# A graph-network layer: messages split around the factors, transfers asked for earlier, the last gate split by tokens

## Chip, cores, metric

One core of a Trainium2 chip runs the whole program, in one launch. The metric is the device time of that program in microseconds (us), median of several executions; lower is better.

## What is computed

The input is x, 32 batches of 512 tokens (nodes) with 256 features, and adj, a 512 by 512 adjacency of zeros and ones for each batch. All is float32. Cut to what matters:

```python
h = relu(layernorm(x))                                # per token
c = relu(bn1(conv1d(h^T, conv1_w)))                   # kernel width 1
c = bn2(conv1d(c, conv2_w, pad=8))                    # kernel width 17, along the tokens
x_conv = relu(c + h^T)^T
s = h @ w_se.T + b_se                                 # 3 features per token
A = exp(-|s_n - s_m|^2) * adj
msg = relu(h @ w_msg.T + b_msg)
x_nmp = A @ msg
gi = concat(x_conv, x_nmp) @ w_ih.T + b_ih            # 512 -> 3*256
gh = h @ w_hh.T + b_hh                                # 256 -> 3*256
r, z = sigmoid(gi_r + gh_r), sigmoid(gi_z + gh_z)
n = tanh(gi_n + r * gh_n)
out = x + (1 - z) * n + z * h
```

## The kernel before, in words

Tokens or features lie on the 128 partitions; 256 features are two chunks (DC = 2), 512 tokens four (NC = 4). The batches form two groups of 16 (GB = 16, NG = 2). For each group the kernel runs a first part and then the nodes; when both groups are done, the late part runs over 16 pairs of batches.

**First part** (`first_part`, manual order). For each batch: load x (`load_x`, most from POOL's queue), layer-norm statistics on VectorE (DVE) with a power on GpSimd (POOL) for rstd, normalise to `xn`, transpose on TensorE to `phT`, relu into `hT`, store `hT` to device memory as `hd` (SP's queue), conv1 as products `pc` into `h1`, and a transform of token windows to frequencies (`px`, copied to `xf`). In group 0 the steps between carry the conv2 weights to frequencies (`pw`, `wst`, `wd`) and load small weights. In group 1 they carry `combine_weights`: the three gate weight matrices are loaded in turn into one buffer `w` (bufs=1), combined on POOL (sums, L886 in the profile) and ScalarE (ACT, copies) into seven matrices each, and stored as `ws`. One step of that list runs per batch, from the second batch on: before the change a list of 13 steps, in which the load of the second and third matrix is the last entry of the step that ends the matrix before.

At the very start the queues are filled in this order: ACT asks for `vec` (vectors), `fwd` (forward transform), `taps`, and four pieces of w1 (`w_in`); SP asks for batch 0 (512 KB, one transfer), batch 1, and the first conv2 weights (`w2p`). TensorE meanwhile runs six products that nobody reads, into `row`. The batch-norm scale of conv1 is turned into rows (`bn1_row`: ACT copies, PE products) and multiplied into w1 by `scale_w1` on DVE.

**Nodes** (`nodes`). The order of the batches is `todo`: the last batch of the group first. `load_h` fetches h again, `by_chunks` copies it into another order (`hq`, ACT), `message` makes `msg` and the three s-features (products `pm`; DVE empties the banks, ACT applies the relu), `features` writes s and its squares into the shared tiles `fl` and `fr` (DVE), `factors` transposes them (`psl`, `psr`) and ACT copies them to `sl` and `sr`, `affinity` multiplies these (`pd`), takes exp on ACT into `e` and multiplies by the transposed adjacency on DVE into A, and `aggregate` makes `pn` from `msg` and A. In between, `product` does the frequency units of conv2 (`py` from weights `wt`, whose sum `wsum` and factor sums `both` POOL makes) and stores `yd`. Before the loop two batches are prepared under a manual order; inside the loop the framework's scheduler sets each engine's order from the program's order. All engines work their own queue strictly in order. `hT` has two slots, `adj` two, `hq` two, `wt` three.

**Late part** (manual order). For each pair of batches the conv2 result comes back from frequencies (`inverse`, `cp`), and the gates are made with a seven-product scheme (Q1 to Q7) in place of eight; `sums` on POOL builds the operands. For the last pair `last_z` runs after `gate_n`: seven products `pz` for z, then for each quarter (output half i, batch j of the pair) `gated` (add on DVE, sigmoid on ACT), `turned` (multiply and transpose on DVE) and `added` (add onto x on DVE), then `store`.

The hardware DMAs of SP and ACT share a set of completion counters, eight in turn, whatever queue they are issued from.

Of the kernel before, what the change touches and what calls it, by code (L numbers as in the profile page):

```python
# [11 lines left out]
FP = mybir.dt.float32  # L12
# [3 lines left out]
P = 128  # L16
# [49 lines left out]
def gnn_layer(  # L66
# [15 lines left out]
    nc = tc.nc  # L82
    B, N, D = x.shape
# [3 lines left out]
    DC = D // P  # L87
# [17 lines left out]
    def bank(name):  # L105
        return psum.tile([P, N], FP, tag="bank", name=name)
# [22 lines left out]
    nc.scalar.dma_start(vec, vecs)  # L129
    w1 = early.tile([P, DC, D], FP, name="w1")  # L130
    fwd = early.tile([P, 2 * L], FP, name="fwd")
    nc.scalar.dma_start(fwd, nc.inline_tensor(fwd_np, name="dft_fwd").ap())
    taps = early.tile([P, ROWS], FP, name="taps")
    nc.scalar.dma_start(taps, nc.inline_tensor(taps_np, name="dft_taps").ap())
    back = consts.tile([P, back_np.shape[1]], FP, name="back")
# [53 lines left out]
    def load_w1():  # L189

        t = W2P["w1"] = pools["gen"].tile([P, PI, D], FP, tag="w2p", name="w1_in", bufs=2)
        load_rows(t[:, :DC], w1T, nc.scalar)

    def scale_w1():
        t = W2P.pop("w1")
# [229 lines left out]
            nc.scalar.copy(chunks(HQ[b][:, ic, :]), by_chunk(HT[b][:, ic, :]))  # L425
        del HT[b]

    def message(b):
        MSG[b] = pools["nodes"].tile([P, NC, D], FP, tag="msg", name=f"msg_{b}", bufs=3)
        ST[b] = pools["nodes"].tile([P, 2, NC, NS], FP, tag="st", name=f"st_{b}", bufs=2)  # L430
        hq = HQ.pop(b)
        h = N // D
        for c0 in range(0, NC, h):
            m = MSG[b][:, c0 : c0 + h, :]
            for j in range(h):
                c = c0 + j
                p = bank(f"pm_{b}_{c}")
                for ic in range(DC):
                    nc.tensor.matmul(p[:, : D + NS], hq[:, ic, c * P : (c + 1) * P], wmsg[:, ic, :],  # L439
                                     start=(ic == 0), stop=(ic == DC - 1))  # L440
                nc.vector.tensor_add(ST[b][:, 0, c, :], p[:, D : D + NS], bmsg[:, D:])
                nc.vector.tensor_add(m[:, j, :], p[:, :D], bmsg[:, :D])
            nc.scalar.activation(m, m, AF.Relu)

    def features(b):

# [62 lines left out]
    def combine_weights():  # L509

        steps = []
        for k, src in enumerate((w_hhT, w_ihT[D:], w_ihT[:D])):
            w, t = (pools["sums"].tile([P, n, 3 * P], FP, tag=f"w{n}", name=f"w{n}_{k}", bufs=m) for n, m in ((4, 1), (7, 2)))
            rows = w.rearrange("p (c h) m -> p c (h m)", c=DC)
            load = (partial(nc.sync.dma_start, rows, src.rearrange("(c p) m -> p c m", p=P)) if k == 1 else
                    partial(load_rows, rows, src, nc.sync))
            if k == 0:
                steps.append([])
            steps[-1].append(load)

            a11, a21, a12, a22 = (
                w[:, 2 * c : 2 * c + 2].rearrange("p h m -> p (h m)").rearrange("p (g i o) -> p g i o", i=2, o=32)[:, :, i]
                for c in range(DC) for i in range(2)
            )
            q = [t[:, n].rearrange("p (g o) -> p g o", o=32) for n in range(7)]
            for (dst, x1, x2, op), kept in zip(
                ((Q5, a21, a22, ALU.add), (Q6, q[Q5], a11, ALU.subtract),
                 (Q7, a11, a21, ALU.subtract), (Q3, a12, q[Q6], ALU.subtract)),
                ((Q1, a11), (Q2, a12), (Q4, a22), None),
            ):  # L530
                steps.append([partial(nc.gpsimd.tensor_tensor, q[dst], x1, x2, op=op)])
                if kept:
                    steps[-1].append(partial(nc.scalar.copy, q[kept[0]], kept[1]))
            steps[-1].append(partial(nc.sync.dma_start, WS[k], t.rearrange("p q (g o) -> p q g o", o=P)))
        return steps
# [113 lines left out]
    def last_z(p, terms):  # L649

        d, o, ks = RZ[p], 1, range(K3)

        def gated(src, other, i, j, t=slice(0, N)):
            z, g = d[:, DC + i, j, t], DC + i
            if other is not None:
                nc.vector.tensor_add(z, other[:, t], src[:, t])
                src = z
            nc.scalar.activation(z, src, AF.Sigmoid, bias=brz[:, g : g + 1], scale=1.0)

        def places(i, t):  # L660
            return slice(t.start // 32, t.stop // 32), slice(32 * i, 32 * (i + 1))

        def turned(i, j, t=slice(0, N)):
            dst, (js, half) = d[:, i, j, t], places(i, t)
            nc.vector.tensor_mul(dst, dst, d[:, DC + i, j, t])
            if (p, j) not in OUT:
                OUT[p, j] = pools["late"].tile([P, N // 32, D // 4], FP, tag="o", name=f"o_{p}_{j}", bufs=2)
            nc.vector.transpose(OUT[p, j][:, js, half], dst.rearrange("p (j k) -> p j k", k=32))

        def added(i, j, t=slice(0, N)):  # L670
            js, half = places(i, t)
            x = XP[p][j][:, js, half]
            nc.vector.tensor_add(x, x, OUT[p, j][:, js, half])

        b1, b2, b3, b4, *b5 = (bank(f"pz{k}_{p}") for k in range(1, 7))
        into(b1, Q1, o, ks, terms, True)
        p1 = temp("p1", f"z{p}")
        nc.scalar.copy(p1, b1)
        into(b2, Q6, o, ks, terms, True)
        u2 = temp("u2", f"z{p}")  # L680
        nc.vector.tensor_add(u2, p1, b2)
        into(b1, Q2, o, ks, terms, False)
        gated(b1, None, 0, 0)
        early_out(p, 1, 1)
        turned(0, 0)
        into(b2, Q7, o, ks, terms, False)
        u3 = temp("u3", f"z{p}")
        nc.vector.tensor_add(u3, p1, b2)
        early_out(p, 0, 1)
        added(0, 0)  # L690
        into(b4, Q4, o, ks, terms, True)
        gated(b4, u3, 1, 0)
        into(b3, Q5, o, ks, terms, True)
        turned(1, 0)
        gated(b3, u3, 1, 1)
        nc.vector.tensor_add(u2, u2, b3)
        added(1, 0)
        store(p, 0, [nc.sync, nc.scalar])

        ts = [slice(h * N // 2, (h + 1) * N // 2) for h in range(2)]  # L700
        into(b5[0], Q3, o, ks, terms, True, ts[0])
        gated(b5[0], u2, 0, 1, ts[0])
        turned(1, 1)
        into(b5[1], Q3, o, ks, terms, True, ts[1])
        gated(b5[1], u2, 0, 1, ts[1])
        added(1, 1)
        for t in ts:
            turned(0, 1, t)
            added(0, 1, t)
            store(p, 1, [nc.sync, nc.scalar], t)  # L710
# [100 lines left out]
    def first_part(g, freq, between, left=()):  # L811
# [6 lines left out]
        if g == 0:  # L818
            t = XN[b0] = pools["first"].tile([P, NC, D], FP, tag="xn", name="rows", bufs=2)
            ones, diags = t[:, 0, :P], t[:, 1:3, :].rearrange("p i (c m) -> p i c m", m=P)  # L820
            nc.vector.memset(ones, 1.0)

            for _ in range(6):
                nc.tensor.matmul(row1[1][:, : 2 * P], ident, fr.rearrange("p c g k -> p (c g k)")[:, : 2 * P], start=True, stop=True)
            batch_norm("bn1", scale1, shift1, nc.gpsimd)
            bn1_row(0, scale1, ones, diags)
            bn1_row(1, shift1, ones, diags)
# [75 lines left out]
    with tc.tile_pool(name="freq", bufs=1) as fpool:  # L903
# [3 lines left out]
        with phase("first", "gen"):  # L907
            gen = pools["gen"]
            per = N // D
            steps = [partial(weights_to_freq, gen, pc, i) for pc in range(QI // PI) for i in range(0, PI, per)]  # L910
            load_w1()
            load_x(0)
            load_x(1)
            load_taps(gen, 0, nc.sync)

            def between(b):
                if b % 2 == 0 and b // 2 + 1 < QI // PI:
                    load_taps(gen, b // 2 + 1)
                if 1 <= b <= len(load_weights):
                    load_weights[b - 1]()  # L920
                mine = spread(steps, b, GB - 1) if b < GB - 1 else []
                return mine[:1], mine[1:]

            with tc.manual_schedule():
                xf = first_part(0, freq_tile, between)

                for u in range(3):
                    load_unit(0, u)
# [4 lines left out]
        def nodes(g, xf, units, last):  # L933
# [11 lines left out]
            load_adj(todo[0])  # L945
            with tc.manual_schedule():
                begin(0)
                message(todo[1])
                factors(todo[0])
                features(todo[1])  # L950
            affinity(todo[0])
            for i, b in enumerate(todo):
# [4 lines left out]
                    load_x(b1)  # L957
                if g + 1 < NG and i == 3 * GB // 4:
                    statistics(b1)
                if i + 2 < GB and todo[i + 2] not in HT:  # L960
                    load_h(todo[i + 2])
                if more:
                    load_adj(todo[i + 1])
                    factors(todo[i + 1])
# [4 lines left out]
                for u in mine[:1]:  # L969
                    product(pools["pw"], g, u, xf)  # L970
                begin(i + 2)
                if more:
                    affinity(todo[i + 1])
                for u in mine[1:2]:
# [109 lines left out]
```

## Time and profile before

| what | value |
|---|---|
| time, median of 7 runs (lowest, highest) | 1847.26 us (1844.19 to 1848.78) |
| profiled execution: time, span | 1848.72 us, 1846.9 us |
| mean granted TensorE clock | 0.995 |
| PE busy, instructions | 1825.8 us (99%), 6610 |
| DVE, ACT, POOL busy | 1110.3 (60%), 582.4 (32%), 588.2 us (32%) |
| group 0: first part, nodes | to about 165 us, to about 460 us |
| group 1: first part, nodes | to about 579 us, to about 880 us |
| late part | from about 880 us to the end |
| last PE product ends, last DVE instruction ends | 1837.8, 1842.6 us |

How to read it: the span is the time from the first to the last instruction of one profiled execution; its time has 1.8 us more around it. Busy time of PE counts the time in which a product is under way, at whatever clock was granted. A row of the timeline has the start, the length, the engine (PEld is PE's weight load; SPq and ACTq are the queues that issue DMAs), the line, the operation, and in brackets the idle time before it with the one who ended it. A row of waits has the total, the number and the longest.

### The profile page before, as it was taken

To read this page: it belongs to the slowest core of one execution; us is meant where nothing else is said; L and a number is where in the kernel's file an instruction comes from. 1 tells how busy PE (TensorE), PEld (TensorE's weight loads), DVE (VectorE), ACT (ScalarE), POOL (GpSimd) and SP (SyncE) were. 2 spreads that over 40 slices of the span, in tenths; PEclk is the share of its full clock that TensorE was granted. 3 is DMA by queue.
4 is the path that set the end of the run, shared out by engine and by line. 5 is a ranking of instruction groups with operands and counts; after the bars stand their busy time and mean duration, and the time that the engine had idled before them with its cause. 6 is when DMAs were issued, how large, how long until landed. Compare 5 with 4: busy or idle time off the path is not lost.

```text
span 1846.9 us, 20105 instructions
## 1 busy us (share of the span) xinstructions
PE 1825.8 (99%) x6610; PEld 1089.3 (59%) x6610; DVE 1110.3 (60%) x2220; ACT 582.4 (32%) x1083; POOL 588.2 (32%) x572
## 2 busy tenths in 40 slices
PE   9999999999999999999999999999999999999998
PEld 6767666666888676665545554555455544555443
DVE  7775656554885545545266466655666566645666
ACT  4555434432335333333222221222122221222121
POOL 3331333333432344444422323133212323133221
PEclk9999999999999999999999999999999999999999
DMA  9999889865678988778421443234422442244412
GB/s 232 303 272 241 222 228 248 218 179 180 212 249 207 242 244 232 222 204 259 122 86 34 120 120 101 56 83 120 120 79 41 120 120 89 50 101 120 113 25 52
DMA packets 307452, 289.26 MB, mean 157 GB/s; under 512 B 148028, under 2 KB 237148, under 8 KB 306964
## 3 DMA queue, kind: packets, MB, share of 16 engines
q1 hardware_dynamic: 281300, 224.22, 46.4%
q10 hardware_dynamic: 19024, 38.68, 5.9%
q0 software_dynamic: 7024, 25.07, 4.9%
q8 instruction: 53, 0.87, 0.2%
q14 instruction: 51, 0.42, 0.1%
HBM read 191.50 MB, written 96.40 MB: 156 GB/s over the span
## 4 chain that ended last, share of the span: by engine, by line
PE 88%; DVE 4%; DMA 3%; issue 2%; POOL 1%; ACT 1%; SPq 0%; POOLq 0%; DVEq 0%; ACTq 0%
PE pg L597 29%; PE pn L597 14%; PE pn L489 11%; PE py L393 11%; PE pm L439 5%; PE pc L585 5%; PE pc L328 4%; PE px L343 2%; PE pw L256 2%; PE pd L474 2%; PE phT L312 1%; DMA w<-in_w_ihT_dram 1%; PE psr L463 1%; DVE stats L285 1%; DMA x<-in_x_dram 1%
## 5 line engine op out<-in xcount | busy, mean ns | idle before, releaser
L489 PE MATMUL pn<-A,msg 128*128 128x512 f32 x512 | 225.9, 593 | 0.7 <-DVE A L480 0.7
L597 PE MATMUL pg<-hp,sw 128*128 128x512 f32 x434 | 221.8, 593 | 0.7 <-DVE rz L616 0.5
L597 PE MATMUL pg<-cp,sw 128*128 128x512 f32 x434 | 221.6, 592 | 0.0
L597 PE MATMUL pg<-np,sw 128*128 128x512 f32 x434 | 221.6, 592 | 0.0
L575 POOL TENSOR_TENSOR hp<-hp 128x512 f32<-128x512 f32 x64 | 81.3, 1280 | 412.7 <-DMA hp<-hd 293.0
L372 POOL TENSOR_TENSOR both<-xf 128x256 f32<-128x256 f32 x78 | 60.5, 776 | 325.1 <-PE py L393 294.3
L489 PEld LDWEIGHTS pn<-A,msg 128*128 128x128 f32 x512 | 97.2, 191 | 111.1 <-issue 105.7
L575 POOL TENSOR_TENSOR cp<-cp 128x512 f32<-128x512 f32 x64 | 80.4, 1267 | 229.7 <-ACT cp L591 228.5
L393 PE MATMUL py<-wt,both 128*128 128x256 f32 x624 | 151.0, 385 | 0.7 <-issue 0.7
L612 ACT ACTIVATE rz<-rz,brz 128x512 f32<-128x512 f32 x93 | 67.0, 722 | 260.2 <-DVE rz L616 260.2
L400 DVE TENSOR_TENSOR y<-y,py 128x256 f32<-128x256 f32 x78 | 31.8, 408 | 189.2 <-ACT y L399 189.2
L597 PEld LDWEIGHTS pg<-hp,sw 128*128 128x128 f32 x434 | 82.2, 190 | 104.7 <-issue 97.6
L597 PEld LDWEIGHTS pg<-np,sw 128*128 128x128 f32 x434 | 82.5, 190 | 103.8 <-issue 103.8
L597 PEld LDWEIGHTS pg<-cp,sw 128*128 128x128 f32 x434 | 82.5, 190 | 103.8 <-issue 103.8
L393 PEld LDWEIGHTS py<-wt,both 128*128 128x128 f32 x624 | 114.2, 190 | 43.2 <-issue 28.3
L480 DVE TENSOR_TENSOR A<-e,at 128x512 f32<-128x512 f32 x128 | 115.0, 937 | 36.6 <-ACT e L477 36.4
L359 POOL TENSOR_TENSOR wsum<-wt 128x512 f32<-128x512 f32 x78 | 108.7, 1395 | 54.1 <-DMA wt<-wd 43.7
L735 ACT ACTIVATE nt<-nt,vech 128x512 f32<-128x512 f32 x64 | 46.2, 722 | 235.8 <-DVE nt L734 235.8
L328 PE MATMUL pc<-w,hT 128*128 128x256 f32 x512 | 118.5, 385 | 1.7 <-DVE hT L316 1.7
L439 PE MATMUL pm<-wmsg,hq 128*128 128x259 f32 x512 | 117.1, 381 | 0.0
L597 PE MATMUL pn<-np,sw 128*128 128x512 f32 x224 | 114.4, 592 | 0.0
L597 PE MATMUL pn<-hp,sw 128*128 128x512 f32 x224 | 114.4, 592 | 0.0
(146 smaller groups left out, 2963.0 us busy)
## 6 DMA issues: line engine op xcount, KB each, us to landing
wt<-wd SPq DMA_DIRECT2D x160, 256.0 KB, 4.4
adj<-in_adj_dram SPq DMA_DIRECT2D x128, 256.0 KB, 5.6
wd<-wst SPq DMA_DIRECT2D x64, 320.0 KB, 5.4
yd<-y ACTq DMA_DIRECT2D x80, 256.0 KB, 4.2
yt<-yd SPq DMA_DIRECT2D x30, 640.0 KB, 7.4
hd<-hT SPq DMA_DIRECT2D x32, 512.0 KB, 4.5
nd<-nmp ACTq DMA_DIRECT2D x32, 512.0 KB, 3.8
xb<-in_x_dram SPq DMA_DIRECT2D x128, 128.0 KB, 3.9
```

The lines of the kernel that those rows point to most:

```text
L328: nc.tensor.matmul(p[:, j, :], HT[b][:, ic, c * P : (c + 1) * P], w1[:, ic, :], start=(ic == 0), stop=(ic == DC - 1))
L359: nc.gpsimd.tensor_tensor(t, WT[g, u][:, 0], WT[g, u][:, 1], op=ALU.add)
L372: nc.gpsimd.tensor_tensor(both[:, 0], re, im, op=ALU.add)
L393: nc.tensor.matmul(dst, v[:, ic, :], w[:, ic, :], start=(ic == 0), stop=(ic == DC - 1))
L439: nc.tensor.matmul(p[:, : D + NS], hq[:, ic, c * P : (c + 1) * P], wmsg[:, ic, :], start=(ic == 0), stop=(ic == DC - 1))
L480: nc.vector.tensor_mul(A[b][:, mc, :], e, at)
L489: nc.tensor.matmul(p, MSG[b][:, mc, dc * P : (dc + 1) * P], A[b][:, mc, :], start=(mc == 0), stop=(mc == NC - 1))
L575: nc.gpsimd.tensor_tensor(t[:, dst, :], t[:, a, :], t[:, b, :], op=sub)
L585: nc.tensor.matmul(bk[:, t0:t1], YT[p][j][:, c, oc * P : (oc + 1) * P], back[:, n : n + t1 - t0], start=(c == 0), stop=(c == len(spans) - ...
L597: nc.tensor.matmul(bk[:, t], sw[:, k, q, o, :], terms[k][q][:, t], start=(first and i == 0), stop=(i == len(ks) - 1), skip_group_check=True)
L612: nc.scalar.activation(rz[:, g, j, :], src, AF.Sigmoid, bias=brz[:, g : g + 1], scale=1.0)
L735: nc.scalar.activation(n, n, AF.Tanh, bias=b_in[:, i : i + 1], scale=1.0)
```

## The change

The first weight products of each node stage are split: of the second batch's four message chunks, two come before the transposes of the first batch's factors and two behind. The h of a batch is asked for one turn of the node loop earlier, later in the turn. In the gate weight list an empty step is put after the second and the third load, so the list has 15 steps and each use comes one batch later. Batch 0 is loaded in four transfers, two from SP and two from ACT; w1 moves from ACT's queue to SP's, and `fwd` from the front of ACT's queue to the end of the first transfers; one of the six unread products is dropped. In `last_z`, Q5 is made in two halves by tokens ahead of Q4, Q3 accumulates into the same two banks, an add on DVE (u2 + b3) falls away, the quarter (1,1) is finished before (1,0), and batch j=0 is stored at the end of these, from SP alone.

```diff
-    nc.scalar.dma_start(fwd, nc.inline_tensor(fwd_np, name="dft_fwd").ap())
...
     def load_w1():
-        load_rows(t[:, :DC], w1T, nc.scalar)
+        load_rows(t[:, :DC], w1T, nc.sync)
...
-    def message(b):
-        MSG[b] = ...
-        ST[b] = ...
-        hq = HQ.pop(b)
-        h = N // D
-        for c0 in range(0, NC, h):
+    def message(b, halves=range(2)):
+        if 0 in halves:
+            MSG[b] = ...
+            ST[b] = ...
+        hq = HQ[b]
+        h = NC // 2
+        for c0 in (h * k for k in halves):
...
+        if 1 in halves:
+            del HQ[b]
...
     def combine_weights():
             steps[-1].append(load)
+            if k > 0:
+                steps.append([])
...
     def last_z(p, terms):
-        b1, b2, b3, b4, *b5 = (bank(f"pz{k}_{p}") for k in range(1, 7))
+        ts = [slice(h * N // 2, (h + 1) * N // 2) for h in range(2)]
+        b1, b2, b4, *b3 = (bank(f"pz{k}_{p}") for k in range(1, 6))
...
         added(0, 0)
+        for bk, t in zip(b3, ts):
+            into(bk, Q5, o, ks, terms, True, t)
+            gated(bk, u3, 1, 1, t)
         into(b4, Q4, o, ks, terms, True)
+        turned(1, 1)
+        added(1, 1)
         gated(b4, u3, 1, 0)
-        into(b3, Q5, o, ks, terms, True)
-        turned(1, 0)
-        gated(b3, u3, 1, 1)
-        nc.vector.tensor_add(u2, u2, b3)
+        for bk, t in zip(b3, ts):
+            into(bk, Q3, o, ks, terms, False, t)
+            gated(bk, u2, 0, 1, t)
+            if t is ts[0]:
+                turned(1, 0)
         added(1, 0)
-        store(p, 0, [nc.sync, nc.scalar])
-
-        ts = [slice(h * N // 2, (h + 1) * N // 2) for h in range(2)]
-        into(b5[0], Q3, o, ks, terms, True, ts[0])
-        gated(b5[0], u2, 0, 1, ts[0])
-        turned(1, 1)
-        into(b5[1], Q3, o, ks, terms, True, ts[1])
-        gated(b5[1], u2, 0, 1, ts[1])
-        added(1, 1)
+        store(p, 0, [nc.sync])
         for t in ts:
             turned(0, 1, t)
             added(0, 1, t)
             store(p, 1, [nc.sync, nc.scalar], t)
...
     def first_part(g, freq, between, left=()):
-            for _ in range(6):
+            for _ in range(5):
                 nc.tensor.matmul(row1[1]...)
...
+            X[0] = pools["first"].tile([P, NC, D], FP, tag="x", name="x_0", bufs=3)
+            for c in range(NC):
+                (nc.sync if c % 2 == 0 else nc.scalar).dma_start(X[0][:, c, :], x[0, c * P : (c + 1) * P, :])
             load_w1()
-            load_x(0)
             load_x(1)
             load_taps(gen, 0, nc.sync)
+            nc.scalar.dma_start(fwd, nc.inline_tensor(fwd_np, name="dft_fwd").ap())
...
     def nodes(g, xf, units, last):
                 begin(0)
-                message(todo[1])
+                message(todo[1], [0])
                 factors(todo[0])
+                message(todo[1], [1])
                 features(todo[1])
...
-                if i + 2 < GB and todo[i + 2] not in HT:
-                    load_h(todo[i + 2])
                 if more:
                     load_adj(todo[i + 1])
                     factors(todo[i + 1])
...
                 begin(i + 2)
+                if i + 3 < GB:
+                    load_h(todo[i + 3])
                 if more:
                     affinity(todo[i + 1])
```

More of the change, by code (lines that the diff above doesn't have):

```diff
@@ L426, in by_chunks @@
         del HT[b]
-    def message(b):
-        MSG[b] = pools["nodes"].tile([P, NC, D], FP, tag="msg", name=f"msg_{b}", bufs=3)
-        ST[b] = pools["nodes"].tile([P, 2, NC, NS], FP, tag="st", name=f"st_{b}", bufs=2)
-        hq = HQ.pop(b)
-        h = N // D
-        for c0 in range(0, NC, h):
+    def message(b, halves=range(2)):
+        if 0 in halves:
+            MSG[b] = pools["nodes"].tile([P, NC, D], FP, tag="msg", name=f"msg_{b}", bufs=3)
+            ST[b] = pools["nodes"].tile([P, 2, NC, NS], FP, tag="st", name=f"st_{b}", bufs=2)
+        hq = HQ[b]
+        h = NC // 2
+        for c0 in (h * k for k in halves):
             m = MSG[b][:, c0 : c0 + h, :]
```

## The prediction, made before the change was run

> **What bounds the kernel now.** I read the page first. Its part 1:
>
> ```profile
> PE 1825.8 (99%) x6610; PEld 1089.3 (59%) x6610; DVE 1110.3 (60%) x2220; ACT 582.4 (32%) x1083; POOL 588.2 (32%) x572
> ```
>
> TensorE is busy for 1825.8 of 1846.9 us, so this change, which takes hardly any product away, can win only from the 21.1 us in which PE idles and from stretches in which it is busy but slow. About 9 us of the idle time is the end (PE stops at 1837.8). The table of waits, TensorE alone, has the rest (the reader is to see that each is a single event of 0.5 to 2 us, not a steady loss):
>
> ```profile
> PE pd L474 <- ACT sr L465: 2.7, 2, 1.3
> PE pc L328 <- DVE hT L316: 1.7, 2, 1.3
> PE phT L312 <- DVE xn L304: 1.4, 1, 1.4
> PE pd L474 <- DVE y L400: 1.4, 1, 1.4
> PE py L393 <- issue: 0.7, 1, 0.7
> ```
>
> Third, the timeline around each. For the gate weights:
>
> ```profile
> 547.16 1.00 POOL L886 TENSOR_TENSOR w<-w 128x384 f32<-128x384 f32 x1 [6.53 <-DMA w<-in_w_ihT_dram]
> 548.92 1.04 POOL L291 TENSOR_TENSOR rstd<-rstd,minus_half 128x4 f32<-128x4 f32 x1
> 550.00 2.13 DVE L304 TENSOR_SCALAR xn<-x,mv,rstd 128x256 f32<-128x256 f32 x4 [2.22 <-POOL rstd L291]
> 551.23 1.72 PE L312 MATMUL phT<-ident,xn 128*128 128x128 f32 x8 [1.44 <-DVE xn L304]
> ```
>
> POOL stands 6.53 us at a gate weight that was asked for in the same step; the next batch's rstd queues behind it, then xn, then PE. For h:
>
> ```profile
> 214.23 0.32 SPq L413 DMA_DIRECT2D hT<-hd  x1
> 218.87 1.14 ACT L425 COPY hq<-hT 128x512 f32<-128x512 f32 x2 [5.65 <-DMA hT<-hd]
> 220.31 0.42 DVE L400 TENSOR_TENSOR y<-y,py 128x256 f32<-128x256 f32 x1 [7.77 <-ACT y L399]
> 220.78 1.58 PE L474 MATMUL pd<-sr,sl 9*128 9x512 f32 x4 [1.39 <-DVE y L400]
> ```
>
> ACT waits for h, DVE for ACT, PE for DVE's banks. Last, stretches with the granted clock, which stands behind the busy times:
>
> ```profile
> 176.00:180.00 4.00, 4.00 (x14) 3.47 (x15) 0.00 (x0) 1.62 (x4) 1.15 (x1) 0.60 1.26 197
> 224.00:226.00 2.00, 2.00 (x6) 1.55 (x6) 2.00 (x4) 1.55 (x3) 1.02 (x2) 0.50 1.01 352
> ```
>
> The third number from the end is the clock. PE shows as busy, at half speed, after the stalls at 174 and 220. Half-speed stretches of some 3.4 us begin near 12.0, 29.0, 175.9 and 223.7, all whole multiples of 3.41 us apart; each costs 1.7 us (3.4 at half speed). The stalls at 551 and 588 are followed by a clock of 1.00, so it depends on where a stall falls.
>
> **Gate weights: -2.8 us.** In the first part of group 1 the conv1 products start at 530.80, 537.36, 543.87, 552.79, 559.39: steps of 6.50 to 6.60, one of 8.92. That one has lost 2.4. The step from 517.30 to 524.20 lost 0.4 in the same way (POOL waited 4.71 at 518.57). The change puts one empty step between each of these two loads and its first use, 6.5 us. The loads do not move (w has one buffer); the uses go to about 520.3 and 547.5, the weights land at 518.5 and 547.1. Both waits go; the second by only 0.4, so a later landing gives up to 1.4 back: bounds -2.8 and -1.4. I take -2.8. The first load (w_hhT) had a step of its own already and is left as it was. Twelve POOL sums of 1.0 us and nine ACT copies of 0.5 are the same in number; the last two sums now fall in steps 14 and 15, where no xn is left to be slowed. But the last sum then stands on POOL behind a wsum that waits for wt until 571.3, so the store of ws (1344 KB, 6.6 us to land) leaves SP at about 573.6 instead of 566.4. Behind it on SP stand one h load, which waits until 578.9 for its slot anyway, and adj: cost nothing; were that cover gone, adj would come about 1 us later.
>
> **h: -4.0 us.** Products of nodes are paced at 17.37 us with two frequency units a batch; pn starts 204.58 and 226.33, 21.75 apart: 4.4 lost (2.7 waiting, 1.7 clock). Asked for a batch earlier, h is there: its slot was freed by the copy of the batch before. What is late next there is wt (POOL's sum ended 214.96, its product starts 222) and adj; neither binds. On SP, h now stands behind adj and in front of some wt instead of ahead of adj; each batch still has one h, four adj and the same wt. Its 512 KB at the 240 GB/s of that stretch can push wt by 2.1 us. Bounds: -4.4 and, if wt then binds once, +2. I take -4.0. The other waits of ACT for h (21.8 us in 8) released no waiting PE: nothing.
>
> **Second messages behind first factors: -1.1 us.** The five transposes (0.27 + 0.60) go ahead of 8 of 16 pm products (3.51/2 = 1.76 us), which cover the copies sl and sr (0.25 + 0.59) and the relu of 0.63 that stands in front of them on ACT. So pd's wait of 1.34 goes, twice. A new wait comes: the second features on DVE end 0.9 later, and the next psl needs them. In group 0 they end at 174.8+0.9 against pd's new end of some 174.4 to 174.9: 0.8 to 1.3 back, since POOL slows DVE there; in group 1 at 588.4 against 588.3. But in group 1 DVE then waits for adj, which does not come sooner:
>
> ```profile
> 589.24 1.31 DVE L479 STREAM_TRANSPOSE at<-adj 128x512 f32<-128x512 f32 x2 [1.74 <-DMA adj<-in_adj_dram]
> ```
>
> and py's 0.7 (597.43) can grow by all that is won. Bounds -2.7 and 0, and -1.7 more if the slow stretch at 176 goes too; I take -0.5 and -0.6, near the middle, as each stall has a known successor.
>
> **Start: -0.3 us.** Conv1 starts at 11.47, after w1:
>
> ```profile
> 10.06 0.75 DVE L197 TENSOR_TENSOR w<-w_in,row 128x256 f32<-128x256 f32 x2 [0.75 <-DMA w_in<-in_w1T_dram]
> ```
>
> and hT behind it on DVE. With w1 early, ACT's hT (ends 10.77) binds: at most -0.65. Against it, SP's waits show that a ninth transfer waits for an early one:
>
> ```profile
> SPq L243 <- DMA vec<-in_vecs_dram: 2.4, 1, 2.4
> SPq L243 <- DMA fwd<-dft_fwd: 1.7, 1, 1.7
> SPq L243 <- DMA taps<-dft_taps: 0.9, 1, 0.9
> ```
>
> With batch 0 as four transfers, two of w1's four pieces come ninth or later. One behind taps (issued about 1.2, 5.6 us) starts at 6.8 and lands by its own 5.7 at 12.5, conv1 at 14.0: +2.5. fwd, now last on ACT, may wait alike, with the table load (1.28) and the copies for row behind it; behind vec (4.1) that is free, behind w1 it lies within the same +2.5. x of batch 0: one 512 KB transfer takes 4.2 us, 128 KB ones 3.9, so the pieces win nothing sure; those on ACT stand behind vec and taps. x of batch 1 and the conv2 taps move behind w1 on SP, wanted at 11.33 and 16.81: covered. One warm-up product less (two records of 0.37) only lengthens an idle 0.68. I take -0.3, near the favourable end because w1 no longer shares the engines with batch 1.
>
> The Trainium skill (DMA: Bandwidth & Descriptors, Bandwidth) speaks against the pieces: it wants transfers of 1 MiB, and its fit of 2.0 us plus bytes over 436 GB/s would give an estimate of 2.3 us for a piece and 3.2 for the whole. By the page the first piece would come 0.9 sooner and the start would go to its bound of -0.65.
>
> **Last z: +0.2 us.** Q5 in halves costs PE nothing (3 pairs of 0.43 or 6 of 0.215: 1.29 us both). DVE loses the 0.67 of L696, and turned(1,1) moves ahead; followed op by op (0.69, 0.71, 0.65 whole; 0.41, 0.45, 0.42 halves) DVE ends about 1842.2 instead of 1842.6. But batch 30 is stored after 1839.6 instead of 1837.5, all on SP: 1.05 MB at the 210 GB/s of 1843 to 1845 then end at 1845.2, where now they end at 1845.1. Bounds -0.5 and +1.5.
>
> **Sum.** -2.8 - 4.0 - 1.1 - 0.3 + 0.2 = -8.0 on the profiled execution (1848.72 us, 1.8 around its span). That execution is 1.5 above the median of 1847.26, and the half-speed stretch inside the h stall need not be in all. I take 1.0 off: 1847.26 - 7.0 = 1840.3.
>
> The Trainium skill (TensorE: Matmul & The Clock Gate, Part 1) has the clock fall after an idle window of some 3.4 us. Here stalls of 1.3 to 1.4 us were enough twice and not twice; by the page h would be worth 2.7 and the sum would be 1841.6 or so.
>
> **Rivals.**
> (a) The stalls only change hands: adj holds the node starts, wt or adj the place of h. Then -2.8 + 0.2 = -2.6: 1844.7, no change by measure (0.2%, 3.7 us, is about what a measurement can tell). For it: the DMA engines are at 0.9 to 1.2 of their time around 170 and 205. Against: PE shows no other wait. 0.18.
> (b) Slower: the moved h load blocks SP. SP already waited 33.9 us in 8 times for ACT's hq at this load, 4.2 each; if h now stands before its slot is free, with wt behind it, wsum and py are late in each of 29 batches. It decides from (8.0+3.7)/29 = 0.4 us a batch; at 0.6 us: 1847.3 - 7 + 17.4 = 1857.7. Against: wt is issued an iteration ahead. 0.08.
> (c) The forecast, 0.74.
>
> All favourable ends together give -0.65-2.7-1.7-4.4-2.8-0.5 = -12.8, 1834.5. The range, 1836.5 to 1845.2, takes in (a) and leaves out (b) and the outer part of the favourable ends.
>
> **What would show it.** Right: no POOL wait for in_w_ihT over 1 us, all conv1 steps of group 1 within 6.5 to 6.9; no ACT wait for hd over 2 us in nodes and pn starts 17.4 or 20.0 apart throughout; pd's wait for sr gone; conv1 at about 11.2; PE's idle 16 to 18 us. Wrong: idle time after pd or py at the node starts as large as before, conv1 after 12, SP waits at L413 in most batches, or a span end more than 10 us after the last product.

## The result and the profile after

The kernel after takes 1839.96 us (median of 17 runs, 1837.66 to 1843.75), the kernel before 1846.66 (41 runs, the seven of the table above among them). The ratio is 0.9965, 95% interval 0.9957 to 0.9973: 6.5 us less, between 5.0 and 7.9. The profiled execution took 1842.02 us with a span of 1840.2 (before: 1848.72 and 1846.9), so the two traces differ by 6.7, and what follows accounts for these 6.7 first.

The page, part 1, of the kernel after:

```profile
PE 1820.5 (99%) x6614; PEld 1086.3 (59%) x6614; DVE 1107.4 (60%) x2220; ACT 582.7 (32%) x1084; POOL 588.4 (32%) x572
```

TensorE is busy for 5.3 us less, although its work is the same but for one warm-up product. Its idle time fell only from 21.1 to 19.7, but it has a longer end in it: ahead of the last product it fell by 3.3 us. So of the 8.6 us won ahead of that product 3.3 were waiting, and most of the rest was slow running. The waits of TensorE after the change (us in all, times, longest):

```profile
PE pm L439 <- ACT hq L424: 1.0, 1, 1.0
PE psl L460 <- DVE fl L453: 0.8, 1, 0.8
...
PE py L392 <- DMA wt<-wd: 0.5, 1, 0.5
PE py L392 <- POOL wsum L358: 0.4, 1, 0.4
...
PE pd L476 <- ACT sr L467: 0.4, 1, 0.4
```

Of pd's 2.7 for sr 0.4 is left, and its 1.4 for y is gone. In what follows the first, second and third pn are the starts of the products `pn` of the first, second and third batch of a group's nodes. Three waits that the page of before did not have stand in front of the second pn of group 0 (timeline, start and duration first, the pause and who ended it in brackets):

```profile
195.06 3.77 PE L439 MATMUL pm<-wmsg,hq 128*128 128x259 f32 x16 [0.98 <-ACT hq L424]
...
201.41 1.10 PE L392 MATMUL py<-wt,both 128*128 128x256 f32 x4 [0.46 <-DMA wt<-wd]
...
202.96 1.13 PE L392 MATMUL py<-wsum,xf 128*128 128x256 f32 x4 [0.44 <-POOL wsum L358]
```

The gate weights: the wait of 6.53 before POOL's sum is gone, but now DVE waits for x, and xn, 1.46 us when nothing runs beside it, takes 2.05 beside the sum:

```profile
545.77 1.40 DVE L284 BATCH_NORM_STATS2 stats<-x 128x6 f32<-128x256 f32 x4 [2.31 <-DMA x<-in_x_dram]
...
548.81 0.98 POOL L890 TENSOR_TENSOR w<-w 128x384 f32<-128x384 f32 x1
548.87 2.05 DVE L303 TENSOR_SCALAR xn<-x,mv,rstd 128x256 f32<-128x256 f32 x4
```

Conv1 starts at 544.54, 551.58 and 558.51: the step of 8.92 became 6.50, but two later ones are 7.04 and 6.93. The start:

```profile
8.97 0.74 DVE L196 TENSOR_TENSOR w<-w_in,row 128x256 f32<-128x256 f32 x2
9.64 0.68 DVE L315 TENSOR_SCALAR hT<-phT 128x512 f32<-128x512 f32 x1
9.92 0.60 ACT L313 ACTIVATE hT<-phT 128x512 f32<-128x512 f32 x1 [1.79 <-PE phT L311]
10.37 3.72 PE L327 MATMUL pc<-w,hT 128*128 128x256 f32 x16 [0.49 <-DVE hT L315]
```

The scaling of w1 (the first line) waits for no transfer any more. But the transfers behind w1 on SP, x of batch 1 and the conv2 weights, now come late, and the second batch's conv1 starts 7.71 us after the first's:

```profile
11.57 1.41 DVE L284 BATCH_NORM_STATS2 stats<-x 128x6 f32<-128x256 f32 x4 [1.26 <-DMA x<-in_x_dram]
14.53 1.20 PE L255 MATMUL pw<-w2p,taps 17*80 17x512 f32 x8 [0.43 <-DMA w2p<-in_w2T_dram]
18.08 3.89 PE L327 MATMUL pc<-w,hT 128*128 128x256 f32 x16 [1.03 <-DVE hT L315]
```

And the end, where the change gives time back. The last product ends at 1829.24 and DVE at 1833.97, 4.7 us apart as before (1837.84 and 1842.60), but the span ends 6.2 us after DVE instead of 4.3:

```profile
1831.45 6.08 SPq L808 DMA_DIRECT2D out_dram<-xb  x8
1832.78 2.97 ACTq L808 DMA_DIRECT2D out_dram<-xb  x4
```

Batch 30's second half is asked for 2.2 us after the last product; before the change it was asked for at 1837.50, 0.34 ahead of it:

```profile
1837.50 5.95 SPq L804 DMA_DIRECT2D out_dram<-xb  x6
1837.50 0.94 ACTq L804 DMA_DIRECT2D out_dram<-xb  x2
```

Cut at seven events, the two traces compare stage by stage; a row begins where the one above it ends. The third and fourth columns are means over the profiled executions of all fourteen kernels of this study, by whether they contain the part (kernels that alter the same stage in another way are left out); the two groups differ in other parts and in clock as well.

| stage | before to after, us | without the part | with it | predicted |
|---|---|---|---|---|
| to the first conv1 product | 11.47 to 10.37: -1.10 | 11.52 (5 traces) | 10.49 (9) | -0.3 for the start |
| to the first pm, group 0 | 154.10 to 154.09: 0.0 | 153.27 (5) | 153.45 (7) | in the same term |
| to the first pn, group 0 (messages) | 21.65 to 19.45: -2.20 | 20.70 (5) | 19.12 (9) | -0.5 |
| first to third pn, group 0 (h) | 39.11 to 37.38: -1.73 | 40.22 (6) | 36.81 (7) | -4.0 |
| to the first pm, group 1 (gate weights) | 352.99 to 350.74: -2.25 | 352.74 (5) | 350.42 (9) | -2.8 |
| to the first pn, group 1 (messages) | 20.78 to 20.00: -0.78 | 21.11 (5) | 19.69 (9) | -0.6 |
| to the last product; of it, second to third pn of group 1 (h) | 1237.74 to 1237.21: -0.53; 20.16 to 19.96 | 21.38 (6), of the latter | 19.96 (7) | 0 |
| last product to end of span (last z) | 9.06 to 10.96: +1.90 | 9.08 (7) | 11.08 (5) | +0.2 |

The 0.0 of the second row is two things that cancel. The clock fell to half speed twice in this stage before and once after, which is 1.7 us less, but the second conv1 came 7.71 after the first instead of 6.35, the interval of eight other traces, three of them without the part. Over the nine traces with the start's part this loss is between 0 and 1.4, 0.4 in the mean.

The second column sums to -6.7. The differences of the means sum to -9.0, more than the timed runs show. One reason is in view: the six profiled executions with the old place of h lay on average 1.9 us above their kernels' medians, the seven with the new one 0.6.

### The profile page after: what moved, and what is told of

Same layout as the page of the kernel before. It is cut to its first block, busy times and chain, and to the rows that moved or that the text cites. A ratio compares the mean times of both kernels' runs of the same rounds, so it can differ in the third digit from the quotient of the medians.

```text
span 1840.2 us, 20108 instructions
## 1 busy us (share of the span) xinstructions
PE 1820.5 (99%) x6614; PEld 1086.3 (59%) x6614; DVE 1107.4 (60%) x2220; ACT 582.7 (32%) x1084; POOL 588.4 (32%) x572
## 4 chain that ended last, share of the span: by engine, by line
PE 65%; issue 1%; DVE 1%; POOL 1%; ACT 0%; DVEq 0%; POOLq 0%; ACTq 0%
PE pg L601 30%; PE pn L601 15%; PE pn L491 6%; PE py L392 6%; PE pc L589 5%; PE pm L439 2%; PE pd L476 1%; PE pz L601 1%; PE psr L465 0%; DVE A L482 0%; POOL cp L579 0%; POOL nt L791 0%; POOL rz L790 0%; DVE at L481 0%; DVE rz L669 0%
## 5 line engine op out<-in xcount | busy, mean ns | idle before, releaser
L601 PE MATMUL pn<-cp,sw 128*128 128x512 f32 x224 | 114.4, 592 | 0.0
```

Of the source, the lines that this page charges most:

```text
L601: nc.tensor.matmul(bk[:, t], sw[:, k, q, o, :], terms[k][q][:, t], start=(first and i == 0), stop=(i == len(ks) - 1), skip_group_check=True)
```

## The experiments

E1 to E5 are the five parts of the change, each alone on the kernel before. The ratio of the whole kernel moves by at most 0.2% in each, with intervals as wide, so they were read by their stages. The kernel before was timed again beside each set of experiments, with medians of 1846.49 (E1 to E4), 1847.94 (E5 to E8), 1845.96 (E9 to E11) and 1846.43 (E12). A difference of two medians from different sets can be off by as much as these differ, so for a comparison with the kernel after (ratio 0.9965) the ratios count.

**E1, the start alone.**

```
- nc.scalar.dma_start(fwd, ...)             (first on ACT)
- load_rows(t[:, :DC], w1T, nc.scalar)      + load_rows(t[:, :DC], w1T, nc.sync)
- load_x(0)                                 + four 128 KB loads of batch 0, SP and ACT in turn
                                            + fwd last on ACT; 5 warm-up products, not 6
```

> The kernel before with the start's part alone (batch 0 in four pieces on two queues, w1 on SP, fwd last on ACT, five warm-up products). Stage theory (each part is worth what its own stage shows between the two traces): conv1 starts at 10.4 instead of 11.5, the first node product 1.1 us sooner (164.5 instead of 165.6), whole kernel -1.1. Rival, coupling: the shift of 1.1 us moves the stall of pd at 174 against the 3.41 us spacing of the half-speed stretches, so the stretches at 176 and 224 go or others come, and the whole kernel is between -4.5 and +1.5, with the difference arising between 165 and 227. Rival, the prediction's term: -0.3.

1845.30 us, ratio 0.9996 (0.9982 to 1.0010). Conv1 at 10.28, first pm at 161.71: 3.9 sooner, not 1.1, since no half-speed stretch fell into the first 200 us. But two in a row stand at 215 to 222 behind the stall for h, and the third pn comes at 222.71 instead of 226.33. So the stage theory holds for conv1, and coupling for the rest: what the start wins passes through stalls and clock, and its whole-kernel worth alone is not separable from none.

**E2, the messages alone.**

```
- message(todo[1]); factors(todo[0])
+ message(todo[1], [0]); factors(todo[0]); message(todo[1], [1])
```

> The kernel before with the message split alone. Stage theory: pd's wait for sr at 174 goes and with it the half-speed stretch at 176, first pn of nodes 2.2 sooner (185.0 instead of 187.2), 0.8 more in group 1, whole kernel -3.0. Rival, stalls change hands: the stall for h in front of the third pn is set by its own transfer and stays at its time, so the 2.2 of group 0 is gone again by the third pn (226.3) and only the 0.8 of group 1 is left. The prediction's term: -1.1 (0.5 and 0.6).

1844.85 us, ratio 0.9990 (0.9975 to 1.0005). From the first pm to the first pn 19.11 instead of 21.65; in group 1 20.11 instead of 20.78. But the third pn comes at 225.65, against 226.33. The stall for h (columns as above):

```profile
216.40 1.14 ACT L425 COPY hq<-hT 128x512 f32<-128x512 f32 x2 [6.10 <-DMA hT<-hd]
...
218.32 2.52 PE L477 MATMUL pd<-sr,sl 9*128 9x512 f32 x4 [1.92 <-DVE y L400]
```

The rival's outcome is right for group 0: alone, most of this part's gain there is gone two batches later. Its reason is not: the stall did not stay at its time, h was asked for 3.6 us sooner (210.65, before 214.23) and pd goes on 2.46 us sooner (218.32, before 220.78). The first pn is 4.2 us sooner, of which 1.25 go to the wait for hq, 0.5 to the stall and 1.8 to the clock: half speed lasts from 218.4 to 225.2 here and reaches only from 223.6 to the third pn before. The first pn interval is 18.61 here and 17.36 in the kernel before; the pm wait for hq (0.98) appears too, so that new wait of the kernel after belongs to the messages, not to h.

**E3, h alone.**

```
- if i + 2 < GB and todo[i + 2] not in HT: load_h(todo[i + 2])     (ahead of load_adj)
+ if i + 3 < GB: load_h(todo[i + 3])                               (behind begin(i + 2))
```

> The kernel before with h asked for a batch sooner, alone. Theory A (the new waits for wt, wsum and hq in front of the second pn come from the transfer of h that now stands ahead of wt): they appear here too, 2 to 2.7 us in front of the second pn, and the part is worth -1.8 to -2.4. Theory B (they come because the other parts let TensorE run ahead of the transfers): none of them here, pn starts 17.4 apart from the first on, worth -4.0 to -4.4 as predicted.

1844.23 us, ratio 0.9983 (0.9970 to 0.9996), -3.1. Both theories hold a part. The interval from the second to the third pn falls from 21.75 to 17.37, and in group 1 from 20.16 (21.10 in E2) to 19.96. But the one from the first to the second grows from 17.36 to 18.77, with waits for the frequency weights that the kernel before did not have:

```profile
202.13 1.10 PE L393 MATMUL py<-wt,both 128*128 128x256 f32 x4 [0.66 <-DMA wt<-wd]
...
203.48 1.13 PE L393 MATMUL py<-wsum,xf 128*128 128x256 f32 x4 [0.24 <-POOL wsum L359]
```

So h ahead of wt costs 1.4 here, and the messages 1.25 by hq (E2); the 2.65 of the kernel after in this interval is both.

**E4, the gate weights alone.**

```
  steps[-1].append(load)
+ if k > 0: steps.append([])
```

> The kernel before with the empty step between each gate-weight load and its first use, alone. Theory A (the sums moved to later steps run beside xn and x now lands late, as in the trace after): two conv1 steps of group 1 near 550 are 6.9 to 7.1 instead of 6.5, whole kernel -2.0. Theory B (those two steps come from other parts of the change): all steps 6.5 to 6.6 and -2.8. Both: no POOL wait for in_w_ihT over 1 us.

1846.04 us, ratio 1.0002 (0.9989 to 1.0016): nothing to be seen in the whole kernel, whose trace has half-speed stretches at 218 to 225 and 586 to 590. The stage itself goes from 352.99 to 351.70, 1.3 us, just less than the prediction's least favourable bound of 1.4. Theory A: the steps 547.89 to 555.40 and 555.40 to 562.34 are 7.51 and 6.94, and DVE waits for x:

```profile
549.59 1.41 DVE L285 BATCH_NORM_STATS2 stats<-x 128x6 f32<-128x256 f32 x4 [2.88 <-DMA x<-in_x_dram]
```

No POOL wait for in_w_ihT over 1 us is left. The wait has passed from POOL to DVE, shortened. How much of it reaches TensorE differs from run to run: in the nine traces with this part the step that waits for x takes 6.50 to 7.51, the next one 6.78 to 6.94.

**E5, the last z alone.**

```
- Q4; Q5 whole, u2 += Q5; store(p, 0, [nc.sync, nc.scalar]); Q3 by halves
+ Q5 by halves; Q4; Q3 by halves into Q5's banks; store(p, 0, [nc.sync])
```

> The kernel before with the last z's part alone (Q5 and Q3 by halves of the tokens, batch 30 stored from SP alone). Theory A (the stores of batch 30 on SP alone are late): DVE still ends 4.7 to 4.8 us after the last product, but the span ends about 6.2 instead of 4.3 us after DVE; whole kernel +1.3 to +1.9. Theory B, the prediction's term (the stores' data end with the rate of the DMA engines whatever the queue): +0.2, span end 4.3 to 4.5 after DVE.

1848.92 us, ratio 1.0006 (0.9992 to 1.0020). DVE ends 4.75 us after the last product and the span 6.45 after DVE, last product to end 11.2. The size is theory A's. Its reason was tested next.

**E6, the kernel after with both queues for that store.**

```
- store(p, 0, [nc.sync])
+ store(p, 0, [nc.sync, nc.scalar])
```

> The kernel after, with batch 30's second half stored from SP and ACT in turn, as before the change. Theory A (SP alone is what makes the end late): the span ends 4.3 to 4.6 us after DVE instead of 6.2, whole kernel -1.6 to -1.9 against the kernel after. Theory B (the DMA engines' rate sets the end): within 0.4 of the kernel after. Rival C: ACT's issues of these stores stand in front of the last sigmoids, DVE ends 0.5 to 1 later and nothing is won.

1840.47 us, ratio 0.9958 (0.9944 to 0.9972), the kernel after within 0.5. The span ends 5.9 after DVE. Theory A falls: the queue is worth 0.3 of the 1.9. Rival C falls too, since DVE ends 4.73 after the last product as before. Theory B is left: the stores of both batches now go out in one lump.

**E7, the kernel after with other products between the small ones at 25 us.**

```
+ if g == 0 and b == b0 + 1: windows_to_freq(b - 1, xf, [0])
  for step in one: step()
+ windows_to_freq(b - 1, xf, [1])          (the whole of it elsewhere, as before)
```

> The kernel after, with half of the frequency products of batch 0 (full 128 rows of the array, 1.2 us) moved between the small products of 17 rows at 25 us, behind which all six profiles so far show half speed at 26 to 31 although TensorE is busy without a pause. Theory A (the clock is judged in windows of 3.41 us by how much of the array works, rows times time, not by pauses; that window has a share of 0.25 to 0.35 now and gets about 0.6): clock 1.00 from 20 to 40, -1.7 us against the kernel after. Theory B (only pauses count, or the drop comes from something else there): the half-speed stretch stays, 0.

(The expectation counts six profiles with that stretch; it was five, E1's had none.) 1838.73 us, ratio 0.9951 (0.9932 to 0.9970); clock 1.00 from 20 to 40. This is what theory A says, but it does not prove it: E1 was spared without the edit, the share of the window (23.0 to 26.4) came out at 0.41 and not 0.6, and the interval reaches over that of the kernel after. Not settled by this run.

**E8, the kernel after with h at the end of the iteration.**

```
- load_h(todo[i + 3])      (behind begin(i + 2))
+ load_h(todo[i + 3])      (behind the last product of the iteration)
```

> The kernel after, with h asked for at the end of the batch's iteration instead of in its middle, so that the transfers of the two frequency weights stand in front of it on SP. Theory A (the waits of 2.65 us in front of the second pn come from the place of h in the queue): the waits for wt and wsum at 201 to 203 go, second pn 18.0 or less after the first instead of 20.0, -1 to -2 us against the kernel after. Theory B (the DMA engines are full there, shares of 0.9 to 1.25, so some transfer is late whatever the order): the waits only change names, within 0.7 of the kernel after, or h is late again at the third pn.

1844.64 us, ratio 0.9976 (0.9959 to 0.9994): above the kernel after by 4.7 by the medians and by 2.0 by the ratios, whose intervals overlap, so this rests on the stages. Theory B, by its second sign: h is late again at the third pn. The first pn interval is 18.61 instead of 20.01, as promised by A, but the second is 24.92:

```profile
216.18 1.14 ACT L424 COPY hq<-hT 128x512 f32<-128x512 f32 x2 [7.21 <-DMA hT<-hd]
...
218.10 2.52 PE L476 MATMUL pd<-sr,sl 9*128 9x512 f32 x4 [3.03 <-DVE y L399]
```

The 1.4 that h costs by standing in front of wt is the price of the 7.6 by which this interval is over 17.37 here; up to 3.4 of these are half speed, from 217.8 to 224.7. In group 1 the same interval is 22.26 instead of 19.96.

**E9, the kernel after without the last z's part** (the old order of E5's diff, everything else kept).

> The kernel after with the last z as it was before (the other four parts kept). Theory A (in the tail the place of batch 30's store is what counts: asked for 2.2 us behind the last product instead of 0.3 ahead of it, so the 1.05 MB of the last two batches go out in one lump): the span ends 8.8 to 9.2 us behind the last product instead of 11.0, whole kernel -1.9 to -2.1 against the kernel after, ratio about 0.9955. Theory B, the prediction's term (the data end at the same time either way): within 0.4 of the kernel after.

1836.85 us, ratio 0.9950 (0.9932 to 0.9968): 3.1 below the kernel after by the medians, 2.8 by the ratios, with intervals that overlap a little. Last product to end 9.30 us against 10.96. Theory A; 1.7 is what the tail itself gives, the rest is within the spread.

**E10, E9 and E7 together.**

> The four parts without the last z, and half of batch 0's frequency products between the small products near 25 us. If the parts add: -2.0 for the tail and, for the clock, half speed at 24 to 31 in about 16 of 34 positions of the 3.41 us windows instead of 28 (so -0.6 to -0.8 on the mean, -1.7 in an execution that is spared), together about 1837.5 median and a ratio near 0.995. If the clock part is worth nothing: as without the last z alone.

1837.72 us, ratio 0.9948 (0.9931 to 0.9964): as E9, so the edit of E7 is worth nothing that these runs show. Half speed now came at 18 to 21, outside the place that the edit protects.

**E11, the kernel after without h's part.**

> The kernel after with h asked for as late as before. Theory A (worth of h is mostly the clock: the single long pause in front of the third pn, next to the products of 9 rows, brings half speed behind it, the scattered pauses after the change do not): from the first to the third pn of group 0 40 to 41 us with a half-speed stretch near 216 to 225, instead of 37.4 with none; whole kernel +3 to +4 against the kernel after. Theory B (the stalls only change hands): 38 or less, whole kernel within +1. The prediction's term: +4.0.

1844.34 us, ratio 0.9990 (0.9976 to 1.0004): 4.4 above the kernel after by the medians, 4.6 by the ratios, whose intervals do not meet. First to third pn 38.89, with a half-speed stretch from 220 to 223.6. That is less than theory A's 40 to 41; but the loss has a second place, which neither theory named: in group 1 the interval from the second to the third pn is 23.79 instead of 19.96, with half speed from 630. Theory B falls.

**E12, the kernel after with Q4 first again.**

```
  into(b4, Q4); gated(b4, u3, 1, 0)
  Q5 by halves; turned(1, 0) behind the first
  added(1, 0); store(p, 0, [nc.sync, nc.scalar])
  Q3 by halves into Q5's banks; turned(1, 1) behind the first
```

> The kernel after with Q4 ahead of the halves of Q5 again, so that batch 30's second half is finished and stored (from SP and ACT) before the halves of Q3; the halves themselves and the missing addition of Q5 to u2 are kept. Theory A (in the last z only the place of batch 30's store costs): the store is asked for 0.3 us or more ahead of the last product, the span ends 8.3 to 9.2 us behind the last product instead of 11.0, whole kernel -1.8 to -2.7 against the kernel after, as much as without the last z's part (1836.9). Theory B (splitting Q5 itself costs): DVE ends over 5.0 us behind the last product, or the stores still go out in one lump, 10 us or more.

1837.67 us, ratio 0.9944 (0.9924 to 0.9964). Theory A: the store is asked for 1.2 us ahead of the last product (1829.59), DVE ends 3.95 after it, the span 8.3 after it, the shortest of all fourteen traces:

```profile
1828.43 5.96 SPq L809 DMA_DIRECT2D out_dram<-xb  x6
1828.44 0.94 ACTq L809 DMA_DIRECT2D out_dram<-xb  x2
```

So the halves of Q5 and the addition saved were worth 0.8 us; putting them ahead of Q4 turned that into a loss of 2. This version is below both kernels by its median, the one before clearly, the one after with intervals that overlap a little.

## Why the prediction was right, and which of its steps were not

The total (1840.3 against 1839.96) and the side were right, and the forecast was nearer than rivals (a) and (b). But that it came within 0.4 us is in part luck: against the trace h was forecast 2.3 us too good and the last z 1.7, the second messages 1.9 too poor and the start 0.8, and these misses nearly cancelled (the trace moved by 6.7 where the sum said 8.0); the 1.0 taken off the sum did the rest.

- **Gate weights, -2.8.** Mechanism right, size near: -2.25, and -2.3 by the means, inside the bounds, but -1.3 alone (E4), just outside. The steps of 8.92 and 6.90 both became 6.50, as forecast. The mis-sized step is what follows "both waits go": the transfer of x became late in place of the weight (DVE waits 2.31, and that step is 0.54 over 6.50), and the sums beside xn, costed at nothing, made it take 2.05 and then 2.74 (the next step is 0.43 over). The steps of 7.04 and 6.93 break the claim of 6.5 to 6.9.
- **h, -4.0.** In the two traces only -1.73; over the traces -3.4 in group 0 and -1.4 in group 1. The stall at the third pn went as predicted (21.75 to 17.37, and 17.37 in all seven traces with the part). The step that failed is "neither binds": wt and its sum bind once, in front of the second pn. It cost 1.4 alone (E3), less than the +2 of the stated bound, and is rival (a) in this one place; the other 1.25 of the loss there is the messages' (E2). The term "the other waits released no waiting PE: nothing" also failed: the wait in group 1 cost 0.2 in the profile that was read, but 1.0 to 1.2 in four other traces with the old order, and 3.8 in E11. One profiled execution had shown the mildest case. The sign "no ACT wait for hd over 2 us in nodes" did not come either: in group 1 ACT still waits four times, 11.6 us in all, 4.6 at most, but pn starts stay 19.96 apart.
- **Second messages, -1.1.** Mis-sized the other way: -2.20 and -0.78, by the means -1.57 and -1.43. The give-back through psl was 0.79, as costed (0.8 to 1.3), but the slow stretch at 176, kept out of the term and named as -1.7 more, went:

```profile
176.00:180.00 4.00, 4.00 (x20) 3.31 (x18) 1.48 (x6) 1.28 (x3) 0.38 (x1) 1.00 1.25 192
```

 The clock is 1.00 where it was 0.60. Not all of this is the change: without the part, E3 and E4 have the same wait of pd (TensorE idle for 1.34 us between 171 and 183) at a clock of 1.00, and their stage takes 20.0 us. Against these the part is worth 0.9 in group 0, nearer to the -0.5; the other 1.6 is a half-speed stretch that comes in some executions only (here before and E5). A give-back of about 1.0 that the prediction did not have came a batch later, at pm for hq; it hides in h's row of the table.
- **Start, -0.3.** Conv1 came at 10.37, beyond the favourable bound of 10.82. Three pieces of the working failed. "128 KB ones 3.9, so the pieces win nothing sure" was the median of the 128 loads of `xb`, far from the start; here (KB each, median us from issue to landing) the two on SP took 2.4:

```profile
x<-in_x_dram SPq DMA_DIRECT2D x2, 128.0 KB, 2.4
x<-in_x_dram ACTq DMA_DIRECT2D x2, 128.0 KB, 3.4
```

 The wait for an early transfer, which was to hold a piece of w1 until 6.8, was 0.4 us (for a piece of x), as taps landed 2.2 us after its issue and not 5.6; so the +2.5 did not come. And "covered", for x of batch 1 and the conv2 taps, failed: with the waits of 1.03 and 0.43 shown above this trace gave back 1.36 of the gain one batch later.

 The Trainium skill (DMA: Bandwidth & Descriptors, Anatomy of one DMA) has the fit from which the estimate of 2.3 us for a piece was worked out, for transfers issued from GpSimd. The two pieces on SP (2.4) agree with it, the two on ACT (3.4) do not. The same page's Bandwidth section wants transfers of 1 MiB or more; here the smaller pieces, together with w1's move, brought conv1 sooner.
- **Last z, +0.2.** The term that was wrong in kind: +1.90, outside its bounds. "DVE ends about 1842.2 instead of 1842.6" counted the saved addition of 0.67, but relative to the last product DVE ends as before (4.73 against 4.76), with a new wait of 0.46 for a sigmoid there. "1.05 MB at the 210 GB/s" took the rate of one stretch of 2 us for that of the whole: from the first store of batch 30 the data needed 1832 to 1838.4, 6.4 us or 165 GB/s. With the store 2.5 us later against the last product, nothing was left to run beside the last batch. E5, E6, E9 and E12 show it: the place of the store, hardly the queue.
- **What was to show it.** PE's idle time is 19.7, not 16 to 18, of which 1.9 is the longer end; the total came out right because the clock made up for the rest. One of the signs named for "wrong" did come: the span ends 10.96 us after the last product. It pointed at the right part.

By the clock rows of the two traces, half speed inside the products cost at most 6.5 us up to the third pn before (13.0 us of products: two stretches in the start, one at 176, most of one at 224) and 1.7 after (3.4 us). About half of the 8.6 us won ahead of the tail is this, and as the messages and the start show, some of it is how the two executions fell. The timed runs say the same more weakly: span times one minus the granted clock is 6.6 to 8.1 us in the means of before (four sets of runs) and 5.1 after, though after has the longer tail, whose idle half-speed time is counted in.

## What to carry to other kernels

Ask of a removed stall what is next in the same queue and one batch later: here wt took over from h, x from the gate weight, hq from sr. Reordering the end of a kernel is priced by when the second-to-last batch's store starts relative to the last product, since a lump of stores cannot hide, whichever queue sends it. And one profile shows one draw of the stalls: a wait worth 0.2 us in it was worth 1 to 4 in five others.

## What the runs showed of the hardware

In these traces the granted clock changes in steps of 3.41 us: the half-speed stretches among the products last 3.41 or 6.83, and those of the kernel before start at 11.97, 29.04, 175.81 and 223.60, which are 5, 43 and 14 such steps apart. Where the steps lie differs from run to run (27.54 in the kernel after). What brings half speed is nearer to how much of the array works than to pauses. In the kernel after, TensorE shows hardly a pause in the window before this fall:

```profile
23.95 3.11 PE L255 MATMUL pw<-w2p,taps 17*80 17x512 f32 x8
```

```profile
24.10:27.50 3.40, 3.35 (x11) 1.21 (x11) 3.37 (x13) 3.40 (x8) 1.24 (x2) 1.00 0.77 264
27.50:30.90 3.40, 3.40 (x15) 3.23 (x13) 2.48 (x6) 1.64 (x4) 0.55 (x1) 0.51 0.95 214
```

The first number after the window and its length is TensorE's busy time, 3.35 of 3.40; the clock, third from the end, is 1.00 in one window and 0.51 in the next. The products there use 17 of 128 rows each. (Eight of them take 1.10 us at 21.90, where four run side by side, and 3.11 here, so "busy" does not mean that the array is full.) Over all fourteen traces (from 4 to 35, 160 to 235 and 535 to 600 us: about 650 windows, 32 of them followed by half speed) I summed the time in which products run times the share of rows that one of them uses. Of the 25 windows with a share under 0.42, 24 were followed by half speed (the other is E7's, 0.41); of all the rest 8, four of these already at half speed. With the rows of products that run side by side added up, the limit moves to 0.49 and sorts as well, 24 of 25. Busy time sorts them badly: of the 28 windows busy for under 70%, 11 were. The limit was read from these same runs, and the exceptions and E7 keep it a regularity, not a proved rule. It fits that the stall beside pd (9 rows) at 174 brought half speed (share 0.29 in that window) and the one at 551 did not (0.58), and that the same stall of pd in E3 and E4, which the windows cut otherwise, did not either (0.42, just above the limit, and 0.51).

The Trainium skill (TensorE: Matmul & The Clock Gate, Part 1) has a free-running window of 3413 ns, which the traces agree with, and a fall after an idle window; here no idle window was needed: windows with 2 us of products out of 3.4 were followed by half speed, and so were some without any pause.
